# Cross attention of a perceiver block: weighted values of two batches in one TensorE block, and an order of instructions that counts changes of tiling

## The chip, the cores and the metric

The kernel runs on one core of one Trainium2 chip. Its time is the device time of one execution in microseconds (us). Before the change it is 3078.98 us, the median of three runs (3071.81, 3078.98 and 3079.72 us). The engines are called as in the profile: PE is TensorE (PEld its weight loads), ACT is ScalarE, DVE is VectorE, POOL is GpSimd, SP is SyncE, whose queue issues most DMAs.

## The reference, cut to what matters

Six layers run one after the other on `x` (64 batches of 64 rows, 256 wide). The change touches the first one alone, a cross attention from the 64 rows of a batch to the 256 rows of its context, with 16 heads of 16:

```
def _L0_xattn_ref(query, keys, values, mask, Wq, bq, Wk, bk, Wv, bv, Wo, bo):
    q = (query @ Wq.T + bq)   # 64 batches x 64 rows, 16 heads of 16
    k = (keys @ Wk.T + bk)    # 64 batches x 256 rows
    v = (values @ Wv.T + bv)
    energy = einsum('bhqd,bhkd->bhqk', q, k)
    energy = where(mask == 0, -1e20, energy)
    attention = softmax(energy / 4, axis=-1)
    out = einsum('bhqk,bhkd->bhqd', attention, v)
    return out @ Wo.T + bo
x = x + _L0_xattn_ref(layernorm(x), ctx, ctx, mask, ...)
```

The five layers after it (a second attention, a cell of six small attentions, a third attention, a recurrence, a feed-forward layer) are computed in stages 2 to 4, whose code is the same in both kernels.

## The kernel before, in words

**Stages and planner.** The kernel has four stages, and stage 1 is the cross attention. Each stage is written as Python generators ("threads"), and a small planner, `Sched`, decides at build time in which order their steps are issued. A thread yields a request: an engine with a duration in ns (`PE(n, cols)`, `ACT(n)`, `DVE(n)`, `POOL(n)`, `Q(kb)` for a DMA), a buffer of a pool, or an event. The planner keeps a model time for each engine. In `run` it takes, among the requests that can start, the one with the earliest model start; ties go to the lower `prio`. A later one with a better `prio` goes first if that `prio` is better by more than `margin` and it could start within `ahead` (a tenth in stage 1) of the first one's duration. The order that results is fixed: on the chip each engine runs its list in that order, and semaphores make it wait where data or a buffer is not there.

**Tilings.** The matmuls of stage 1 come in three tilings of the array: `PE` is the whole array (projections, transposes), `PR` uses four row groups of 32 (scores: heads' products with 32 contraction rows), `PC` four column groups of 32 (weighted values). `switch` (line 63) gives what the planner charges for a change of tiling: `s.change`, 0 in stage 1 before the change. In `run`, `aware` adds that charge to a candidate's start `t` before it is compared, and `stick` is added to the sorting key `d` for those candidates that would change the tiling:

```
t = max(t, self.eng[self.OF[o[0]]]) + self.aware * self.switch(o[0])
d = t + self.stick * (self.switch(o[0]) > 0)
cand.append(((d, th.prio, d + o[1]), th, o, t))
```

**A unit.** Stage 1 runs over 32 units of two batches. `unit(u)` (prio 10u + 1) loads the context rows, transposes them (line 385), makes keys and values (`values`, lines 344 to 346 by way of `mm3`), and `keep` stores the transposed context for a later stage. `qgroup` makes the queries of two units. `attend(u)` (prio 10u + 2) spawns `batch(u, 0)` and `batch(u, 1)`, then transposes the result (line 790), divides by the softmax sums (796, 797), transposes again (801), and multiplies by the output weights (`mm3`).

**A batch.** `batch` makes the scores twice. First scores: four mask matmuls (line 712) and eight score matmuls (715), then the row maximum on DVE (719). The maximum is negated and split (723, 724), transposed (727) and copied (730). Second scores, now with keys along the partitions: four matmuls that add the negated maximum (736), sixteen of scores (741), then two exponentials on ACT (753) into `pT`. Then it waits for the unit's values and multiplies: 32 matmuls (line 765) of 128 x 32 weights with 64 columns into the first 256 columns of a PSUM buffer of the pool `b1`, and one copy of 128x256 to the half of `o` that belongs to this batch (769, on ACT or DVE, whichever the planner finds free first). An fp32 matmul shows as two instructions in the trace, so these 32 show as 64.

**Buffers.** The scores have one PSUM buffer (`scp`, four of the eight banks): a scores block can begin only when the maximum or the two exponentials of the block before have read it. `b1` has the four other banks. `pT` has three buffers. Work for stage 2 (`prepare2`, prio 100, context projections) is planned among the units from about the tenth on; it changes the tiling too, as half of its matmuls have 64 contraction rows, but the planner counts them as `PE`.

Of the kernel before, what the change touches and what calls it, by code (L numbers as in the profile page):

```python
# [186 lines left out]
def PE(n, cols=512):  # L187
    return "PE", n * PE_NS.get(cols, max(108.7, cols / 2.4))
# [6 lines left out]
def ACT(n, ap=0):  # L195

    return "ACT", 0.833 * n + 55 + 93 * ap


def DVE(n, ap=0):  # L200
    return "DVE", 1.042 * n + 66 + 61 * ap
# [6 lines left out]
def POOL(n):  # L208
    return "POOL", 2.9 * n + 30


def Q(kb=64, wait=True):

    return "Q", 640.0, kb * 2.84, wait
# [82 lines left out]
def f(ap):  # L297
    return ap.bitcast(F32)
# [41 lines left out]
def mm3(k, out, lhs, rhs, start=True, stop=True):  # L340

    n = len(lhs)
    for i, ((ah, al), (bh, bl)) in enumerate(zip(lhs, rhs)):
        k.nc.tensor.matmul(out, ah, bh, start=start and i == 0, stop=False)  # L344
        k.nc.tensor.matmul(out, ah, bl, start=False, stop=False)  # L345
        k.nc.tensor.matmul(out, al, bh, start=False, stop=stop and i == n - 1)  # L346
# [134 lines left out]
def stage1(k, x_in, x_out, ctx, ctxT, mask, wq, bq, wk, bk, wv, bv, wo, bo, beside, nu=32):  # L481
# [1 line left out]


    nc, tc, s = k.nc, k.tc, k.s
    s.ahead, s.margin = 0.1, 4
    es = ExitStack()
    with es:
        pool = lambda name, bufs, **kw: es.enter_context(tc.tile_pool(name=name, bufs=bufs, **kw))
# [4 lines left out]
        b1 = Buf(k, es, "b1", P1["b1"], [128, 512], F32, PSUM)  # L494
        def weight(tp, n, w):
            W[n] = yield from load_wT(k, wp, tp, b1, "w" + n, w, 256, 256)
            s.set(wev[n])
# [94 lines left out]
        ptp = Buf(k, es, "pT", P1["pT"], [128, 2, 4, 2, 128])  # L592
# [11 lines left out]
        def either(n, ap, act, dve):  # L604
            if (yield [ACT(n, ap), DVE(n, ap)]) == "ACT":
                act()
            else:
                dve()
# [94 lines left out]
        rows = [slice(32 * i, 32 * i + 32) for i in range(4)]  # L703
        two = [slice(32 * i, 32 * i + 2) for i in range(4)]

        def batch(u, b, o):
            g, gb = u // 2, 2 * (u % 2) + b
            q_, k_ = qm[g], kc[u]

            sc = yield from scp.on(("PR", 1350))  # L710
            for i in range(4):
                nc.tensor.matmul(sc[:, i], ones[two[i]], mr[g][two[i], gb].unsqueeze(1).to_broadcast([2, 2, 256]), start=True, stop=False)
            for m in range(2):
                for i in range(4):
                    nc.tensor.matmul(sc[:, i, 256 * m:256 * m + 256], q_[rows[i], m, gb].rearrange("p q s -> p (q s)"),  # L715
                                     k_[rows[i], m, 256 * b:256 * b + 256], start=False, stop=m == 1)
            mx = sp.tile([128, 2, 4], F32, name="mx")
            yield DVE(2048)
            nc.vector.tensor_reduce(mx, sc.rearrange("p i (m s) -> p m i s", m=2), AX.X, ALU.max)  # L719
            scp.rel()  # L720
            nx = yield from nxr.get()
            yield "DVE", 200
            nc.vector.tensor_scalar(nx[:, :, :, 0], mx, -1.0, None, ALU.mult)
            nc.vector.scalar_tensor_tensor(nx[:, :, :, 1], mx, -1.0, f(nx[:, :, :, 0]), ALU.mult, ALU.subtract)
            ps = yield from b1.on(PE(2, 128))
            for m in range(2):
                nc.tensor.transpose(ps[:, 128 * m:128 * m + 128], f(nx[:, m].rearrange("p i r -> p (i r)")), k.ident)
            nr = yield from nrp.get()
            pv, nv = ps[:, 0:256], nr.rearrange("p m s -> p (m s)")
            yield from either(256, 0, lambda: nc.scalar.copy(nv, pv), lambda: nc.vector.tensor_copy(nv, pv))  # L730
            b1.rel()
            nxr.rel(k, nx)

            sc = yield from scp.on(("PR", 1350))
            for i in range(4):
                nc.tensor.matmul(sc[:, i], ones[two[i]], nr[two[i]].unsqueeze(1).to_broadcast([2, 2, 2, 128]), start=True, stop=False)
            for c in range(2):
                for m in range(2):
                    for i in range(4):
                        x0 = 256 * c + 128 * m  # L740
                        nc.tensor.matmul(sc[:, i, x0:x0 + 128], k_[rows[i], m, 256 * b + 128 * c:256 * b + 128 * c + 128],  # L741
                                         q_[rows[i], m, gb].rearrange("p q s -> p (q s)"), start=False, stop=c == 1 and m == 1)
            nrp.rel()
            if b == 1:
                kcp.rel()
            qleft[g] -= 1
            if qleft[g] == 0:
                qmp.rel()
                mrp.rel()
            pT = yield from ptp.get()  # L750
            for c in range(2):
                yield ACT(1024, 1)
                nc.scalar.activation(pT[:, c].rearrange("p i m s -> p i (m s)"), sc[:, :, 256 * c:256 * c + 256], AF.Exp,  # L753
                                     bias=W["mc"][:, c, 2 * u + b:2 * u + b + 1], scale=0.25)
            scp.rel()
            yield vready[u]
            v = vv[u]

            av = (yield from b1.on(("PC", 1300)))[:, 0:256].rearrange("p (a s) -> p a s", a=4)
            for a in range(4):  # L760
                for c in range(2):
                    for j in range(4):
                        h = 4 * a + j
                        x0 = 64 * (h % 2)
                        nc.tensor.matmul(av[rows[j], a], v[:, 2 * b + c, h], pT[:, c, h // 2 % 4, h // 8, x0:x0 + 64],
                                         start=c == 0, stop=c == 1, tile_position=(0, 32 * j))
            ptp.rel()
            ov = o[:, :, b]
            yield from either(256, 0, lambda: nc.scalar.copy(ov, av), lambda: nc.vector.tensor_copy(ov, av))
            b1.rel()  # L770

        def attend(u):
            yield qready[u // 2]
            yield kready[u]
            yield mready[u // 2]
            xo = yield from xop.get()
            yield Q(128, False)
            k.dma(xo, x_in[u * 128:(u + 1) * 128])
            yield wev["o"]
            yield POOL(256)  # L780
            nc.gpsimd.tensor_tensor(xo, xo, W["br"], ALU.add)
            o = yield from otp.get()
            ths = [s.spawn(batch(u, b, o), prio=s.curprio() + 0.1 * b) for b in range(2)]
            for t in ths:
                yield t
            vvr.rel(k, vv[u])

            ps = yield from b1.on(PE(4, 128))
            for a in range(4):
                nc.tensor.transpose(ps[:, 128 * a:128 * a + 128], o[:, a].rearrange("p b s -> p (b s)"), k.ident)  # L790
            otp.rel()
            pv = ps.rearrange("p (h d) -> p h d", d=32)
            r = sp.tile([128, 16], F32, name="r")
            on = yield from op.get()
            yield "DVE", 480
            nc.vector.reciprocal(r, pv[:, :, 16])
            nc.vector.tensor_tensor(on, pv[:, :, 0:16], r.unsqueeze(2).to_broadcast([128, 16, 16]), ALU.mult)
            b1.rel()
            ps = yield from b1.on(PE(2, 128))
            for c in range(2):  # L800
                nc.tensor.transpose(ps[:, 128 * c:128 * c + 128], on[:, 8 * c:8 * c + 8].rearrange("p h d -> p (h d)"), k.ident)
            op.rel()
            ohl = yield from ohp.get()
            oh, ol = ohl[:, 0], ohl[:, 1]
            yield from split_ps(k, oh, ol, ps[:, 0:256].rearrange("p (c s) -> p c s", c=2), 256)
            b1.rel()
            wh, wl = W["o"]
            ps = yield from b1.on(PE(6, 256))
            mm3(k, ps[:, 0:256], [(oh[:, c], ol[:, c]) for c in range(2)], [(wh[:, c], wl[:, c]) for c in range(2)])
            ohp.rel()  # L810
            yield DVE(256)
            nc.vector.tensor_tensor(xo, ps[:, 0:256], xo, ALU.add)
            b1.rel()
            yield Q(128)
            k.dma(x_out[u * 128:(u + 1) * 128], xo)
            xop.rel()
            s.set(k.done1[u])

        def main():
# [6 lines left out]
            for t in ths:  # L826
# [6 lines left out]
        ths = [s.spawn(g, prio=p) for g, p in ((weight(tp, "k", wk), -1), (heads(tp), 0), (weight(tp, "v", wv), 1.2),  # L833
                                               (masks(tp), 1.4), (output(tp), 2.5))]
# [1491 lines left out]
```

## Time and profile before

| | us |
|---|---|
| median of three timed runs | 3078.98 |
| profiled execution, time of the run | 3068.5 |
| its span, first to last instruction | 3066.6 |
| stage 1, from the start to the last output matmul at about 668.7 | 668.7 |
| first scores block starts | 36.7 |
| last scores block starts | 659.1 |
| PE busy, share of the span | 2825.0 (92%) |

Besides the page, the profile answers with groups of instructions by line in a window, busy time in stretches, waits (who waited for whom), and a timeline of instructions in order of time. A matmul's duration is its time through the array, so the time that it costs is read from the distance of two starts and not from its duration. In the timeline consecutive matmuls of one line are merged into one row, and a row's second column runs to the end of the last of them. The granted TensorE clock was 1.00 from 64.2 to 671.8 us.

### The profile page before, as it was taken

The numbers are of one execution on the slowest core, as the hardware profiler recorded it, in microseconds if no ns is written. First come the engines' busy times: TensorE is split into PE (matmuls) and PEld (weight loads), VectorE is DVE, ScalarE is ACT, GpSimd is POOL, SyncE is SP. The second block draws the span as 40 slices with busy tenths as digits, with TensorE's granted clock in tenths as the row PEclk, the third lists the DMA queues.
The fourth block names the chain that finished last, engine by engine and source line by source line (L and its number), as shares of the span: only waits on it lengthen the run. The fifth ranks groups of instructions, "written<-read, shape, count | busy, mean of one in ns | idle before, by whom it ended". The sixth has DMA issues, their size and how long they took to land. (4 is left out here: it accounts for less than half of the span.)

```text
span 3066.6 us, 85592 instructions
## 1 busy us (share of the span) xinstructions
PE 2825.0 (92%) x36849; PEld 2283.0 (74%) x36849; DVE 2278.8 (74%) x3430; ACT 1854.2 (60%) x2849; POOL 1032.0 (34%) x1512
## 2 busy tenths in 40 slices
PE   8999999979999999999998998998889899778888
PEld 7877787856666667666667888988888899556767
DVE  6766665558898888987885787888888778776664
ACT  5554455547776776876774565666556566445553
POOL 3110121124554544544451125234523522441220
PEclk9999999999999999999999999999999999889999
DMA  4433452239998999989995456556555656652220
GB/s 149 126 109 100 131 175 71 72 88 222 179 189 187 203 200 191 203 180 175 172 192 126 114 124 148 138 138 160 148 113 134 144 119 164 165 202 83 76 76 22
DMA packets 916987, 437.66 MB, mean 143 GB/s; under 512 B 774264, under 2 KB 884464, under 8 KB 916352
## 3 DMA queue, kind: packets, MB, share of 16 engines
q1 hardware_dynamic: 916608, 432.18, 60.0%
q8 instruction: 290, 4.75, 0.6%
q14 instruction: 89, 0.73, 0.1%
HBM read 183.30 MB, written 64.23 MB: 81 GB/s over the span
## 5 line engine op out<-in xcount | busy, mean ns | idle before, releaser
L1122 ACT ACTIVATE e<-sc,mx,cst 128x1024 f32<-128x1024 f32 x256 | 306.7, 1199 | 118.5 <-POOL mx L1118 116.6
L1624 POOL TENSOR_TENSOR e<-e,sm 128x1024 f32<-128x1024 f32 x96 | 187.7, 1956 | 500.8 <-DVE sm L1622 347.2
L1131 DVE SCALAR_TENSOR_TENSOR p<-e,rs,p 128x1024 f16<-128x1024 f32 x256 | 326.7, 1288 | 38.9 <-ACT p L1129 37.9
L1116 DVE TENSOR_REDUCE mx<-sc 128x1 f32<-128x1024 f32 x256 | 309.2, 1218 | 55.5 <-PE sc L346 54.6
L1129 ACT ACTIVATE p<-e,rs 128x1024 f16<-128x1024 f32 x256 | 289.2, 1145 | 63.7 <-POOL rs L1126 55.1
L1118 POOL TENSOR_SCALAR mx<-mx,cst 128x1 f32<-128x1 f32 x256 | 179.1, 700 | 260.7 <-DVE mx L1116 257.6
L1180 PE MATMUL av<-pT,vv 128*128 128x256 f16 x1536 | 184.8, 278 | 21.3 <-DMA pT<-p 21.1
L1180 PEld LDWEIGHTS <-vv 128*128 128x128 f16 x1536 | 151.2, 100 | 56.3 <-DMA pT<-p 12.5
L719 DVE TENSOR_REDUCE mx<-sc 128x8 f32<-128x2048 f32 x64 | 146.4, 2288 | 62.2 <-PE sc L715 62.0
L1180 PE MATMUL av<-pT,f 128*128 128x256 f16 x1536 | 181.8, 274 | 10.0 <-DMA pT<-p 8.9
L1180 PEld LDWEIGHTS <-f 128*128 128x128 f16 x1536 | 150.1, 98 | 37.4 <-DMA pT<-p 10.3
L753 ACT ACTIVATE pT<-sc,mcol 128x1024 f32<-128x1024 f32 x128 | 139.0, 1115 | 62.8 <-PE sc L741 62.8
L670 POOL TENSOR_TENSOR cT<-chl 128x1024 f32<-128x1024 f32 x32 | 76.4, 2388 | 256.5 <-issue 174.2
L1126 POOL TENSOR_TENSOR rs<-rs,mone 128x1 f32<-128x1 f32 x256 | 154.1, 602 | 21.3
L364 POOL TENSOR_SCALAR ln_rs<-ln_mv 128x1 f32<-128x1 f32 (+2 forms) x136 | 39.2, 288 | 333.9 <-DVE ln_mv L362 310.3
L1125 POOL TENSOR_SCALAR rs<-rs 128x1 f32<-128x1 f32 x256 | 77.4, 302 | 188.7 <-ACT e L1122 177.9
L460 DVE COPY pT<-pX 128x1024 uint16<-128x1024 uint16 x110 | 119.2, 1098 | 22.6 <-DMA pX<-p 22.2
L458 ACT COPY pT<-pX 128x1024 uint16<-128x1024 uint16 x82 | 111.7, 1362 | 37.9 <-DMA pX<-p 37.2
L1618 ACT ACTIVATE e<-e 128x1024 f32<-128x1024 f32 x96 | 101.5, 1058 | 48.8 <-DVE e L1615 48.3
L1621 DVE TENSOR_REDUCE sm<-e 128x16 f32<-128x1024 f32 x96 | 116.5, 1214 | 19.3 <-ACT e L1618 18.8
L1648 PE MATMUL sc<-pT,vn 64*32 64x64 f32 x6144 | 83.6, 227 | 46.2 <-ACT pT L458 12.0
L1612 DVE TENSOR_REDUCE mx<-sc 128x16 f32<-128x1024 f32 x96 | 115.8, 1206 | 13.7 <-PE sc L1606 5.8
(580 smaller groups left out, 9552.9 us busy)
## 6 DMA issues: line engine op xcount, KB each, us to landing
cn<-in_ctx SPq DMA_DIRECT2D x64, 512.0 KB
f<-wdr SPq DMA_DIRECT2D x60, 512.0 KB
wt<-wdr SPq DMA_DIRECT2D x60, 512.0 KB
ctxT<-cT SPq DMA_DIRECT2D x32, 512.0 KB
cT<-ctxT SPq DMA_DIRECT2D x32, 512.0 KB
wdr<-xh SPq DMA_DIRECT2D x30, 512.0 KB
x<-xo SPq DMA_DIRECT2D x64, 128.0 KB
nate<-in_L_ffn_We SPq DMA_DIRECT2D x18, 256.0 KB
```

Source lines behind the costliest of these rows:

```text
L460: k.nc.vector.tensor_copy(out, in_)
L719: nc.vector.tensor_reduce(mx, sc.rearrange("p i (m s) -> p m i s", m=2), AX.X, ALU.max)
L753: nc.scalar.activation(pT[:, c].rearrange("p i m s -> p i (m s)"), sc[:, :, 256 * c:256 * c + 256], AF.Exp, bias=W["mc"][:, c, 2 * u + b:2 ...
L1116: nc.vector.tensor_reduce(mx, sc, AX.X, ALU.max, negate=True)
L1118: nc.gpsimd.tensor_scalar(mx, mx, esc, None, ALU.mult)
L1122: nc.scalar.activation(e, sc, AF.Exp, bias=mx, scale=esc, accum_out=rs)
L1126: nc.gpsimd.tensor_tensor(rs, rs, mone, ALU.pow)
L1129: nc.scalar.activation(p[:, 0], e, AF.Copy, scale=rs)
L1131: nc.vector.scalar_tensor_tensor(p[:, 1], e, rs, p[:, 0], ALU.mult, ALU.subtract)
L1180: nc.tensor.matmul(out, vv[h][:, c, b], pT[:, a, c], start=n == 0, stop=n == 23)
L1621: nc.vector.tensor_reduce(sm, e, AX.X, ALU.add)
L1624: nc.gpsimd.tensor_tensor(e, e, sm.unsqueeze(3).to_broadcast([128, 4, 4, 64]), ALU.mult)
```

## The change

`batch` ends after the exponentials and leaves its `pT` in a dictionary. A new thread step, `weighted`, runs in `attend` when both batches are done: it waits for the unit's values, takes one `b1` buffer, does the 32 matmuls of batch 0 and then the 32 of batch 1 into all 512 columns of it, and copies 128x512 in one instruction. The planner is told 2300 ns for it where it was told 1300 ns for each batch. The number and shapes of the matmuls are the same.

The first line of the stage gives the planner new settings: `margin` 0 for 4, and a charge of 150 ns for a change of tiling, which is part of a candidate's start (`aware`), with `stick` -150. The durations told for scores (1350) stay.

```
-    s.ahead, s.margin = 0.1, 4
+    s.ahead, s.margin, s.aware, s.change, s.stick = 0.1, 0, True, 150, -150
...
-        def batch(u, b, o):
+        def batch(u, b, pts):
...
             scp.rel()
+            pts[b] = pT
+
+        def weighted(u, pts, o):
+
             yield vready[u]
             v = vv[u]
-            av = (yield from b1.on(("PC", 1300)))[:, 0:256].rearrange("p (a s) -> p a s", a=4)
-            for a in range(4):
...
-            ptp.rel()
-            ov = o[:, :, b]
-            yield from either(256, 0, lambda: nc.scalar.copy(ov, av), lambda: nc.vector.tensor_copy(ov, av))
+            ps = yield from b1.on(("PC", 2300))
+            av = ps.rearrange("p (a b s) -> p a b s", a=4, b=2)
+            for b in range(2):
+                for a in range(4):
+                    for c in range(2):
+                        for j in range(4):
+                            h = 4 * a + j
+                            x0 = 64 * (h % 2)
+                            nc.tensor.matmul(av[rows[j], a, b], v[:, 2 * b + c, h], pts[b][:, c, h // 2 % 4, h // 8, x0:x0 + 64],
+                                             start=c == 0, stop=c == 1, tile_position=(0, 32 * j))
+                ptp.rel()
+            ov = o.rearrange("p a b s -> p (a b s)")
+            yield from either(512, 0, lambda: nc.scalar.copy(ov, ps), lambda: nc.vector.tensor_copy(ov, ps))
             b1.rel()
...
-            ths = [s.spawn(batch(u, b, o), prio=s.curprio() + 0.1 * b) for b in range(2)]
+            pts = {}
+            ths = [s.spawn(batch(u, b, pts), prio=s.curprio() + 0.1 * b) for b in range(2)]
             for t in ths:
                 yield t
+            yield from weighted(u, pts, o)
```

## The prediction

> **What bounds it now.** I read the page first, for the slices, then the busy time in stretches of stage 1, then the waits and timeline there. Stage 1 ends near 668.7 us of a span of 3066.6; in the page's slices that is about the first nine digits.
>
> ```profile
> span 3066.6 us, 85592 instructions
> ...
> PE   8999999979999999999998998998889899778888
> ...
> DVE  6766665558898888987885787888888778776664
> ACT  5554455547776776876774565666556566445553
> ```
>
> In the next answer the columns are the stretch, its length, and the busy time of PE, PEld, DVE, ACT and POOL.
>
> ```profile
> 60.00:561.60 501.60, 490.92 (x7864) 394.20 (x7862) 314.66 (x542) 266.73 (x423) 87.51 (x75) 1.00 0.37 117
> 561.60:596.70 35.10, 34.19 (x619) 28.82 (x612) 18.61 (x27) 19.55 (x31) 6.21 (x4) 1.00 0.23 78
> 640.00:668.60 28.60, 19.17 (x475) 15.46 (x468) 8.96 (x17) 11.01 (x15) 0.10 (x1) 0.92 0.04 12
> ```
>
> PE is busy 98% of the time from 60 to 561.6, ACT 53% and DVE 63%. So PE's list bounds the stage, and what counts is PE's own work plus its few waits. 561.6 to 596.7 is two units without work of stage 2: 17.55 us a unit. The last 28.6 us are a tail in which nothing is left to fill PE.
>
> The waits from 60 to 668 have these two as the longest (total us, times, longest); together with the same two on DVE's maximum (3.7 and 2.3) they are 16.2 us.
>
> ```profile
> PE sc L736 <- ACT pT L753: 7.1, 9, 1.5
> ...
> PE sc L712 <- ACT pT L753: 3.1, 4, 1.3
> ```
>
> PE waits for the one scores buffer. The durations that hold it, from the groups by line:
>
> ```profile
> L719 DVE TENSOR_REDUCE mx<-sc 128x8 f32<-128x2048 f32 x62 | 141.8, 2288 | 62.1 <-PE sc L715 62.0
> L753 ACT ACTIVATE pT<-sc,mcol 128x1024 f32<-128x1024 f32 x124 | 134.7, 1115 | 60.8 <-PE sc L741 60.8
> ```
>
> Either 2.29 us, or twice 1.115 us, lies between two scores blocks, and PE needs other work meanwhile. The timeline shows both sides (start, duration to the last end, idle before):
>
> ```profile
> 607.14 1.04 PE L385 MATMUL b<-ident,cn 128*128 128x128 f32 x8
> 608.83 0.50 PE L736 MATMUL sc<-nr,ones 2*128 2x512 f32 x4 [0.66 <-ACT pT L753]
> 609.17 1.06 PE L741 MATMUL sc<-qm,kc 32*128 32x128 f32 x32
> 610.16 1.10 PE L765 MATMUL b<-pT,vv 128*32 128x64 f32 x64
> 611.19 1.09 PE L385 MATMUL b<-ident,cn 128*128 128x128 f32 x8
> 612.54 0.51 PE L712 MATMUL sc<-mr,ones 2*128 2x512 f32 x4 [0.25 <-ACT pT L753]
> ```
>
> Two second-scores blocks follow each other at 4.06 us, then a first-scores block at 3.71. The weighted values of batch 0 (L765) are fill here, and even with them PE ran dry.
>
> **Merging the weighted values.** A block of 64 instructions costs 1.03 us (610.16 to 611.19). By the single starts in the trace, groups of four start 0.056 us apart, so 16 groups are 0.90 us and 0.135 us is the price of the block: 0.04 at its beginning and 0.09 behind its last group.
>
> ```profile
> 630.28 0.40 PE L345 MATMUL b<-chl,wkh 128*128 128x512 f32 x1
> 630.51 0.40 PE L346 MATMUL b<-chl,wkl 128*128 128x512 f32 x1
> 630.84 1.10 PE L765 MATMUL b<-pT,vv 128*32 128x64 f32 x64
> 631.87 0.51 PE L712 MATMUL sc<-mr,ones 2*128 2x512 f32 x4
> ```
>
> The 0.09 is the change of tiling: siblings start 0.23 apart (630.28, 630.51), the first one of the other tiling 0.33 later. The same 0.09 stands behind scores blocks (0.200 to the next block, where groups are 0.112 apart). From 60 to 668 us I count 61 blocks of weighted values. 55 of their 122 sides touch a scores block; there the array would have changed anyway. So they add 122 - 55 = 67 changes. Afterwards there are 32 blocks with 64 sides. If all stand alone they add 64 changes (3 fewer, 0.3 us), if each touches one scores block 32 (35 fewer, 3.2 us); at today's share of 45% they add 35 (32 fewer, 2.9 us). The 0.04 goes 32 times: 1.3 us. **PE's own work falls by 1.6 to 4.5 us; I take 4.2.** The scores blocks number 128 as before.
>
> **One eviction.** Today 46 copies on ACT at 0.372 us and 18 on DVE at 0.424: 24.7 us. Copies of 128x512 in the same stage (values, line 661) take 0.586 on ACT and 0.689 on DVE; 23 and 9 of them are 19.7. Both engines save 5.0 us together, beside PE's list: nothing on the path. It comes 0.21 to 0.27 us later for the transposes behind it, which wait for it 1.0 us in all today; in the tail there is no cover, so 0.2 us once.
>
> The Trainium skill, "TensorEngine Tiling (Array Packing)", Performance Considerations, PSUM Bottleneck, speaks against this edit: it wants both ScalarE and VectorE to empty PSUM, and one wide copy lets only one do so. The row bears on it with 0.372 against 0.586; if the transposes stood on the path, the rule would make it 32 x 0.21 = 7 us lost, and by the waits it is nothing.
>
> **The added wait.** Batch 0's weighted values used to be issued while batch 1's exponentials ran, and were fill (610.16 above). Now they come behind batch 1's exponentials. Behind them on PE is whatever the planner put there, above all the next unit's first scores. No DMA and no other queue is touched; SP and POOL get nothing new. Two `pT` stay held for some 4 us longer, and the third is free for the next unit's batch 0, so no new wait there.
>
> What it costs depends on who goes first when the exponentials end. Three distances of a unit's four are 3.80, 4.0 and 4.05 at their shortest, and the fourth is 3.71 if the next scores go first. Then the chain through the scores buffer is 15.6 us a unit, below PE's work (17.55 less the 0.45 of waits, 1.8 us in four units, less 0.13: 16.97), and the waits vanish: 0.58 a unit gained here. Over the stage that is at most the 8.8 us that PE waits at lines 712 and 736 from 60 to 630 us. If the merged block goes first, the chain is 15.6 + 1.93 = 17.5, above PE's work: 0.05 gained. In the trace the weighted values precede the next first scores in 25 units of 32 and follow them in 7. The code says why: the scores' start has no latency on the buffer's release, the weighted values' has 250 ns, but a PE that is still filling makes them equal, and then the lower prio, the older unit's, wins. Some 23 units lie outside the work of stage 2, nine inside, where PE has fill and gains its 0.13. **All first: 23 x 0.05 + 9 x 0.13 = 2.3 us gained; all behind: 8.8 + 4.2 = 13.0; weighed 25 to 7: 4.6, so 5.**
>
> **The settings.** They add and remove no instruction. `stick` of -150 takes the 150 out of the key again, so the order is not pulled towards fewer changes; only the planner's clock runs slower. `margin` 0 lets values of a unit precede its own scores within a tenth of a block. Scores cost 1.30 to 1.33 us plus 0.09, 1.42; they were charged 1.35 and are now charged up to 1.65. The merged block costs 2.0 and is charged up to 2.6. Against that, a projection of 512 columns is charged 0.213 and takes 0.23. Over a unit today's plan is 16.65 us against 17.55 real; the new one adds 4 x 0.30 = 1.2, 17.85 against some 17. Errors in both directions of like size: I take 0, with rival 2 below as one end and the 8.8 us of waits, all gone, as the other.
>
> **Sum.** 5 us off: 3068.5 - 5 = 3063.5 for the profiled execution (span 3066.6 and 1.9 around it). The three timed runs have their median 10.5 above it, so 3079.0 - 5 = 3074.0. About 0.3% (9.2 us) is what a measurement of this kernel can tell from no change.
>
> **Rivals.** (1) *Next scores go first.* The chain drops out and 13 us are gained, 3066. For it: the 250 ns, and seven units today. Against it: a full PE hides the 250 ns. (2) *The plan believes in a slower PE than the chip has.* Then the planned fill between two scores blocks is too short and PE waits at lines 712 and 736. Surplus in the fill per unit: 4 x 0.12 (two changes at 150 for 90) + 0.5 (merged block) = 1.0; projections charged too low give back 8% of some 8.6 us fill, 0.7. It decides from the point where the planned fill is down to the wait itself, as at 607.14. 0.3 x 32 = 10 us, 3089; without the giving back 32 us. (3) *The change doesn't do what it says:* the order is as before, apart from the merging, and only the 1.6 to 4.5 us come; that lies in the forecast. Stages 2 to 4 inherit other model times at stage 1's end, so their order can shift a little; I allow 5 us to either side.
>
> **Chances.** Forecast with (3), within 0.3%: 0.46. Rival 1, faster: 0.34. Rival 2, slower: 0.20. The range: down to rival 1 with 5 us of later stages and 5 of scatter between runs, 3056; up to rival 2 with 2 more, 3091. The forecast's own range is 3067 to 3081.
>
> **What would show it.** L765 in 32 blocks of 128, each about 1.93 us to the next start; copies at line 769's successor 0.59 or 0.69; 128 scores blocks; some 30 fewer changes of tiling. Units without stage 2's work at 17.4 to 17.5 us (rival 1: 17.0; rival 2: 17.8 and more, with waits of PE at 712 and 736 well over 16 us). It would be wrong if stage 1 shrank and a later stage grew, or if the tail of 28.6 us changed by more than 1 us.

## The result, and the profile after

| | before | after |
|---|---|---|
| median of 20 timed runs each, us | 3078.6 (3070.8 to 3085.2) | 3083.1 (3078.3 to 3096.9) |
| profiled execution: time, span, us | 3068.5, 3066.6 | 3082.8, 3081.0 |
| last output matmul of stage 1, us | 669.1 | 671.3 |
| mean granted clock | 0.980 | 0.975 |

The ratio is 1.0019, with a 95% interval of 1.0010 to 1.0028: 0.2% slower, within the 0.3% that one measurement can tell from no change, but with 20 runs on each side clearly not the 5 us faster that were forecast. The two profiled executions lie 14 us apart; before's lies 10 us under its median. Two executions of kernels that end behind stage 1 (2039.6 us of after, 2037.8 us of merging alone) took three times as long as the others of the same kernel and are left out of the medians below.

The page of the changed kernel first (slices of 77.0 us; stage 1 is the first nine). PE's first nine digits are those of before, so the answer must be in shorter stretches.

```profile
span 3081.0 us, 85536 instructions
...
PE   8999999979999999999988999999999899778888
```

The stretches that answer to those of before (length; busy time of PE, PEld, DVE, ACT, POOL; granted clock, DMA share, GB/s). The last is a stretch of the same 28.6 us at the stage's end, moved with it.

```profile
60.00:561.60 501.60, 489.70 (x7751) 395.83 (x7749) 302.14 (x534) 264.61 (x409) 92.16 (x76) 1.00 0.38 118
561.60:596.90 35.30, 34.35 (x614) 28.91 (x614) 19.05 (x31) 17.72 (x27) 6.61 (x5) 1.00 0.18 63
642.60:671.20 28.60, 20.12 (x446) 16.05 (x443) 9.43 (x17) 10.93 (x14) 0.10 (x1) 0.88 0.04 12
```

PE is busy 97.6% of the time from 60 to 561.6, nearly as before (97.9%), two units without work of stage 2 take 35.3 us where they took 35.1, and the clock of the last 28.6 us is 0.88 where it was 0.92. The waits of PE from 60 to 668 us (total us, times, longest):

```profile
PE sc L712 <- ACT pT L753: 6.5, 5, 2.3
PE sc L736 <- DVE mx L719: 4.9, 6, 1.7
PE sc L712 <- DVE mx L719: 3.4, 8, 0.5
PE sc L736 <- ACT pT L753: 3.2, 5, 1.3
PE b L770 <- ACT pT L753: 2.2, 3, 1.2
PE b L770 <- issue: 1.6, 2, 1.4
```

The four scores rows add up to 18.0 us, against 16.2 before, and two rows are new, of the merged block (line 770; the lines behind the change are shifted by up to 7): 2.2 us for exponentials, and 1.6 in the middle of two blocks that the profile puts down to nothing ("issue"). The wait for the scores buffer has not gone. What moved is its place. The single copy of 128x512 is there as well, always on ACT:

```profile
L774 ACT COPY ot<-b x32: 585/585/588, 55.3 to 667.1; 128x512 f32<-128x512 f32 x32
```

**How stage 1 divides.** The next table is worked out from the traces, and most of what follows rests on it. "Start" is the first scores block; the body runs from there to the first scores of the 61st batch, the tail from there to the stage's last output matmul. "Idle" is time with no matmul in PE. "Half clock" is time with a granted clock of 0.5 (half of it is taken as lost). "Own work" is the body less its idle time less half of its half-clock time. Each row is a mean over the profiles of all runs with that stage 1, whole or cut off behind it.

| stage 1 (profiles) | start | body | own work | idle | half clock | tail | tail's half clock | end |
|---|---|---|---|---|---|---|---|---|
| before (5) | 37.2 | 595.3 | 578.6 | 15.4 | 2.7 | 38.0 | 8.7 | 670.6 |
| after (4) | 35.5 | 596.4 | 576.6 | 17.8 | 3.9 | 39.7 | 12.3 | 671.5 |
| merging alone (2) | 38.1 | 596.8 | 574.6 | 19.7 | 5.1 | 39.5 | 10.8 | 674.3 |
| settings alone (4) | 35.6 | 592.9 | 579.7 | 12.0 | 2.6 | 37.0 | 4.1 | 665.4 |
| late, not merged (1) | 38.5 | 594.3 | 580.1 | 12.5 | 3.4 | 38.1 | 3.4 | 670.8 |
| behind (1) | 34.9 | 612.0 | 572.5 | 29.2 | 20.5 | 41.5 | 14.9 | 688.4 |
| charge alone (1) | 36.7 | 612.5 | 582.4 | 25.0 | 10.2 | 41.6 | 20.5 | 690.7 |
| margin alone (1) | 35.3 | 607.1 | 578.1 | 22.2 | 13.7 | 41.0 | 18.4 | 683.4 |

Own work and idle time repeat within 1 to 2 us from profile to profile of one kernel; the half-clock time does not (before's tail has 4.8 to 11.8 us). Of the kernels that end behind stage 1, the profiled execution of after, of merging alone and of settings alone was the longest of those timed, so the ends of these three rows lie rather late.

### The profile page after: what moved, and what is told of

It is laid out like the page before. It is cut to its first block, busy times and chain, and to the rows that moved or that the text cites. A ratio compares the mean times of both kernels' runs of the same rounds, so it can differ in the third digit from the quotient of the medians.

```text
span 3081.0 us, 85536 instructions
## 1 busy us (share of the span) xinstructions
PE 2831.8 (92%) x36849; PEld 2292.2 (74%) x36849; DVE 2267.3 (74%) x3428; ACT 1846.5 (60%) x2819; POOL 1037.2 (34%) x1512
## 5 line engine op out<-in xcount | busy, mean ns | idle before, releaser
L1136 ACT ACTIVATE p<-e,rs 128x1024 f16<-128x1024 f32 x256 | 289.2, 1145 | 67.1 <-POOL rs L1133 56.7
L1187 PE MATMUL av<-pT,f 128*128 128x256 f16 x1536 | 184.4, 276 | 12.5 <-DMA pT<-p 11.9
L1187 PEld LDWEIGHTS <-vv 128*128 128x128 f16 x1536 | 151.0, 100 | 57.8 <-DMA pT<-p 13.7
L458 ACT COPY pT<-pX 128x1024 uint16<-128x1024 uint16 x82 | 111.7, 1362 | 35.9 <-DMA pX<-p 35.5
L460 DVE COPY pT<-pX 128x1024 uint16<-128x1024 uint16 x110 | 117.8, 1085 | 20.3 <-DMA pX<-p 19.7
L1619 DVE TENSOR_REDUCE mx<-sc 128x16 f32<-128x1024 f32 x96 | 115.7, 1206 | 13.8 <-PE sc L1613 5.9
```

The source lines that it names most:

```text
L460: k.nc.vector.tensor_copy(out, in_)
L1136: nc.scalar.activation(p[:, 0], e, AF.Copy, scale=rs)
L1187: nc.tensor.matmul(out, vv[h][:, c, b], pT[:, a, c], start=n == 0, stop=n == 23)
L1619: nc.vector.tensor_reduce(mx, sv, AX.X, ALU.max)
```

## The experiments

**Each half alone.** The merged block with the old settings, the new settings with weighted values batch by batch, and the kernel before once more as a control, all beside the kernel before (29 runs, median 3079.3).

```
-    s.ahead, s.margin, s.aware, s.change, s.stick = 0.1, 0, True, 150, -150
+    s.ahead, s.margin = 0.1, 4
```

> The merged block alone, with the planner's settings of before (margin 4, no charge for a change of tiling). Theory A (the merged block is the loss: the fill of batch 0's weighted values is gone and 1.93 us stand ahead of the next scores, so the chain through the scores buffer is as long as PE's work, and in the tail PE idles and its clock falls): stage 1 ends 1 to 3 us later than before (669.1), some 671; time +0 to +0.2%. Theory B (the settings are the loss, the merging gains what was worked out): stage 1 ends 4 to 5 us earlier, 664 to 665, time -0.15%. Theory C (stage 1 is equal, the difference is scatter of the later stages): stage 1 within 1 us of 669.

Measured: 3084.8 us (12 runs, 3080.2 to 3091.9), ratio 1.0016 [1.0007, 1.0024]. Merging alone makes the kernel slower, though PE's own work in stage 1 falls by 4.0 us (578.6 to 574.6). Stage 1 ended at 674.4 us in its profile, later than any of the three theories had it; theory A has the direction.

> The settings alone (margin 0, charge 150 in the start, stick -150), weighted values batch by batch as before. Theory A: stage 1 within 1 us of 669. Theory B: 6 us later or more, some 675, with more waits of PE at lines 712 and 736 than the 16 us of before; time +0.2% or more. Theory C: within 1 us of 669.

Measured: 3081.2 us (12 runs, 3071.9 to 3086.1), ratio 1.0003 [0.9992, 1.0014]: no difference in full time, though stage 1 ends some 5 us earlier (664.0 in its profile). None of the three theories expected that.

> The kernel before, once more, as a measure of scatter: ratio 1.000 within 0.1%. Stage 1 ends at 669.1 within 1 us in every theory; the rest of the span (2397.5 in the first profile, 2409.7 in the changed kernel's) shows how far stages 2 to 4 scatter when nothing is changed. Theory C expects a spread of 5 us and more there.

Measured: 3079.7 us (12 runs), ratio 1.0001 [0.9992, 1.0010]. Its profile has the same order as the one shown and yet a span of 3072.7 against 3066.6. Two profiles of one kernel can lie 6 us apart, so single spans decide nothing here.

**Rival 1 forced: next scores first.** The merged block becomes a thread of its own with a prio behind the next unit's scores.

```
-            yield from weighted(u, pts, o)
+            yield s.spawn(weighted(u, pts, o), prio=s.curprio() + 10.5)
```

> The changed kernel with the merged block in a thread of its own whose prio is worse than that of both batches' scores of the next unit (10.5 more), so that it is fill between scores blocks instead of standing ahead of them. Theory A: units without stage 2's work fall from 17.6 to about 17.0 us, waits at 712 and 736 before 630 us fall from 9.9 to under 5, stage 1 ends 6 to 10 us earlier than the changed kernel's 671.3, at 661 to 665. Theory B (too slow a clock in the plan): the waits stay, stage 1 within 2 us of 671.

Measured: 3093.4 us (6 runs, 3084.8 to 3102.2), ratio 1.0044 [1.0028, 1.0061]. In its order the merged block stands behind the next unit's first scores in 23 units and ahead in 8, of the 31 that have a next unit, where after has 11 and 20. The waits did not vanish: idle time of the body is 29.2 us, the highest of all, and stage 1 ends at 688.4 us, far behind what either theory expected.

**Stage 1 by itself.** The kernel ends behind stage 1, whose result is written out; stages 2 to 4 are left out. The work for stage 2 that is planned among the units stays.

```
-        ps[2] = prepare2(k, x1, *g("L0_attn_", "context Wq Wk Wv Wout bout"))
+        ps[2] = prepare2(k, xo, *g("L0_attn_", "context Wq Wk Wv Wout bout"))
...
-    stage1(k, x0, x1, a["ctx_1024"], ctxT, a["mask_BxS2_ik0"], *g("L0_xattn_", "Wq bq Wk bk Wv bv Wo bo"), before2)
-    stage2(k, x1, x2, ps[2], before3)
-    stage3(k, x2, x3, ps[3], before4, last3)
-    stage4(k, x3, xo, a["ctx_1024"], ctxT, ps[4])
+    stage1(k, x0, xo, a["ctx_1024"], ctxT, a["mask_BxS2_ik0"], *g("L0_xattn_", "Wq bq Wk bk Wv bv Wo bo"), before2)
+    k.e2.close()
```

> The kernel before, cut off after stage 1 (stages 2 to 4 are left out, stage 1 writes to the output). This and the next three time stage 1 alone, without the scatter of the 2400 us behind it. In the two full profiles stage 1 ended at 669.1 and 671.9; I expect a time of 671 to 675 with a spread of about 2 us. Both theories use it as the base.

> The changed kernel, cut off after stage 1 in the same way. Theory D (stage 1 itself is longer, and that is the whole of the +4.5 us): 4 to 5 us over the cut kernel before. Theory E (stage 1 is nearly equal, as the profiles have it, and most of the loss comes behind it although the instructions there are the same): 0 to 2 us over it.

> The new settings alone, weighted values batch by batch, cut off after stage 1. Theory D: equal to the cut kernel before within 2 us, as the full times were. Theory E: 5 to 7 us under it, as the profile of the full kernel has it, so that the gain is lost behind stage 1.

> The merged block alone with the old settings, cut off after stage 1. Theory D: 5 to 6 us over the cut kernel before, as the full times were; theory E: 3 to 5 us over it, as the profile has it.

Measured (medians of four or five): before 675.5 (674.8 to 676.0), after 673.9 (673.0 to 676.1), settings alone 671.7 (670.3 to 675.1), merging alone 678.6 (677.4 to 679.5). (The expectations further down were written with 674.5 and 678.8, medians that counted the two long executions, and so with 2.8 for the cost of merging.) So in stage 1 the settings gain 3.8 us with the old block (675.5 to 671.7) and 4.7 with the merged one (678.6 to 673.9); the merging costs 3.1 with the old settings and 2.2 with the new ones. After is 1.6 us ahead of before here, so the 4.5 us of full time are not lost in stage 1: theory D has fallen, and theory E is the nearer one.

**Up to the end of stage 2.** As before, with stage 2 kept and stages 3 and 4 left out.

```
+    stage1(k, x0, x1, a["ctx_1024"], ctxT, a["mask_BxS2_ik0"], *g("L0_xattn_", "Wq bq Wk bk Wv bv Wo bo"), before2)
+    stage2(k, x1, xo, ps[2], before3)
```

> The kernel before, cut off after stage 2 (stages 3 and 4 are left out, stage 2 writes to the output). With the full times (before 3079.3, after 3083.1, settings alone 3081.2) and the cuts after stage 1 (675.5, 674.5, 671.7), 5 us of the change's loss lie behind stage 1. Base of the next two; I expect 1650 to 1670.

> The changed kernel, cut off after stage 2. Theory E1 (the loss behind stage 1 lies at the start of stage 2, where SyncE's queue and the transfers of pT have a pace of their own and the profiles show 3.6 us lost up to 120 us into the stage): 3 us and more over the cut kernel before. Theory E2 (it lies in stage 3): 1 us under it to 1 us over it, as after stage 1.

> The settings alone, cut off after stage 2. Theory E1: the 3.8 us gained in stage 1 are gone, within 1 us of the cut kernel before. Theory E2: they are still there, 3 to 4 us under it.

Measured: 1643.7 (1637.5 to 1645.0), 1645.3 (1641.1 to 1647.2), 1629.9 (1629.5 to 1631.7). After is 1.6 us behind, with ranges that overlap, so E1 and E2 are not told apart; the settings alone are 13.8 us ahead here, which neither expected, and yet 2 behind at the end of the kernel. Of the 12.3 us between the two profiled spans 8.5 stood at the end of stage 1 already (672.3 and 663.8); where the rest was gained was not traced.

**Up to the end of stage 3.** Stage 4 alone is left out.

```
-    stage3(k, x2, x3, ps[3], before4, last3)
-    stage4(k, x3, xo, a["ctx_1024"], ctxT, ps[4])
+    stage3(k, x2, xo, ps[3], before4, last3)
```

> The kernel before without stage 4 (the recurrence's output is written out instead). It gives the base for the two others of this call: full time 3079 less stage 4's 361 us and the end's, some 2712 to 2722.

> The changed kernel without stage 4. Theory S (the loss of some 5 us behind stage 1 arises in stage 3, with the same instructions, from TensorE's granted clock, which falls at different moments): 4 us above the kernel before cut in the same way, since it stood 1.6 above at the end of stage 2. Rival L (it arises behind stage 3): within 2 us of it.

> The kernel with the new settings and weighted values batch by batch, without stage 4. At the end of stage 2 it stood 13.8 us below before, in full time 1.9 above. Theory S: the 14 to 16 us are lost again in stage 3, so it lies within 3 us of the kernel before cut in the same way, in all of its timed runs. Rival L: some 13 us below.

Measured: 2723.7 (2723.3 to 2727.6), 2729.7 (2726.9 to 2731.1), 2726.0 (2715.1 to 2735.7). Rival L has fallen: after has lost 6.1 us by the end of stage 3 against 1.6 at the end of stage 2, and the settings alone have given all of their 13.8 back by the median. By these medians both go in stage 3. Theory S asked that all runs of the settings alone lie within 3 us of before; they lie from 8.6 below to 12.0 above it.

**The tail.** The last two units with weighted values batch by batch, the others merged; cut off behind stage 1.

```
+            if u < nu - 2:
+                return
+            yield vready[u]
...
-            yield from weighted(u, pts, o)
+            if u < nu - 2:
+                yield from weighted(u, pts, o)
```

> The changed kernel cut off after stage 1, with the weighted values of the last two units batch by batch as before. Theory F (half of the 2.8 us that merging costs under the new settings comes from the tail, where PE idles 2.3 us before two scores blocks and its clock is halved for 6.8 us): 671.5 to 673.5 against 674.5, the tail behind the 60th batch's first scores 37 to 38 us against 39.5. Against it (the tail is bound by the scores buffer alone): 674 to 675.

Measured: 676.5 us (673.0 to 679.0) against 673.9: no gain. The trace says why this run can't decide: both gaps of 2.31 us ahead of the next first scores are still there (632.66 and 650.12). The first needs the block of the third unit from the end, which is still merged in this run. Into the second the planner did not put batch 0's block; it stands ahead of the second scores at 646.41 and delays them.

**The wait without the merging.** Weighted values wait for both batches, but stay two blocks with two copies; old settings; cut off behind stage 1.

```
+            for b in range(2):
+                av = (yield from b1.on(("PC", 1300)))[:, 0:256].rearrange("p (a s) -> p a s", a=4)
...
-            ps = yield from b1.on(("PC", 2300))
```

> The kernel is cut off behind stage 1, with the old settings; the weighted values wait for both batches as after the change, but stay two blocks of 64 with two copies of 128x256. Theory W (the wait costs, the merging saves as forecast): the kernel lacks the some 4 us of PE's work that one block per unit saves, and has the late batch 0, so it lies some 7 us above before's 675.5, at 681 to 684, and some 4 above the merged one's 678.8. Rival E (the wide block is the trouble: 1.93 us that fit badly between two scores blocks, and a copy of 0.59 us): about before's 675.5, within 1.5. Rival N (the late batch 0 costs 3 and the merging saves nothing that reaches the end): within 1 of 678.8.

Measured: 675.5 us (674.2 to 676.1), the same as before. Theory W has fallen, and so has rival N: the wait of batch 0 costs nothing on balance, and what costs is the wide block (with its one copy, and with 2300 ns told for it in place of twice 1300, which this run does not separate from it). The waits of PE in the body, from 36 to 631 us, first of the merged kernel, then of the one with two late blocks:

```profile
PE sc L712 <- ACT pT L753: 6.3, 9, 1.9
PE b L770 <- issue: 3.3, 2, 2.6
```

```profile
PE sc L736 <- DVE mx L719: 3.6, 7, 1.0
PE sc L712 <- ACT pT L753: 3.4, 7, 1.3
```

With two blocks PE has no wait at the weighted values, and the next first scores wait half as long for the exponentials. Own work is 580.1 against 574.6 (the merging saves 5.5 here), idle time 12.5 against 19.7.

The idle time of the body can be sorted by what PE has between two scores blocks (us, in brackets the number of such stretches; one profile each, the first three of kernels that end behind stage 1):

| between two scores blocks | before | two late blocks | merging alone | settings alone | after | behind |
|---|---|---|---|---|---|---|
| weighted values between two first-scores blocks | 0.0 (5) | 0.2 (27) | 4.7 (15) | 0.0 (3) | 4.2 (9) | 13.0 (22) |
| second scores, then first scores, no weighted values between | 1.3 (2) | 5.1 (16) | 7.8 (16) | 2.0 (4) | 4.8 (10) | 6.7 (22) |
| all other stretches | 14.2 | 7.2 | 6.9 | 9.7 | 8.4 | 9.5 |

Lateness has its price in the second row, where the weighted values are missing, and two narrow late blocks make it good elsewhere. What the merged block adds is above all the first row. Not all of that is lack of fill: 2.6 us of the 4.7 and 1.4 of the 4.2 are a single stop inside a merged block that the profile puts down to nothing.

**The settings one by one.** Weighted values as before the change, cut off behind stage 1.

```
-    s.ahead, s.margin = 0.1, 4
+    s.ahead, s.margin, s.aware, s.change, s.stick = 0.1, 4, True, 150, -150
```

> Cut off behind stage 1; weighted values as before the change; of the settings the charge of 150 with its -150 in the key alone, margin 4 as before. If the slower clock of the planner is what gains (it plans less fill between two scores blocks than PE has room for, so the scores come earlier): 671.7 within 1, as with both settings. If it is the margin: 675.5 within 1.

```
-    s.ahead, s.margin = 0.1, 4
+    s.ahead, s.margin = 0.1, 0
```

> Cut off behind stage 1; weighted values as before the change; margin 0 alone, no charge. If the charge is what gains: 675.5 within 1. If the margin is what gains: 671.7 within 1. If each gives a part, the two parts of this run and the one with the charge alone add up to 3.8.

Measured: 695.0 us (693.4 to 696.4) and 690.1 us (688.6 to 691.7), against 675.5 with neither and 671.7 with both. None of the three expectations holds: alone they cost 19.5 and 14.6, together they gain 3.8. With the charge alone the body has 9.6 us more idle time than before's, 3.8 more own work, 3.8 more lost to half clock, and the tail is 3.6 longer. The idle time isn't spread evenly (start, duration, idle before):

```profile
362.16 0.41 PE L801 MATMUL b<-ident,o 128*128 128x128 f32 x2 [1.82 <-DVE o L797]
364.26 0.80 PE L712 MATMUL sc<-mr,ones 2*128 2x512 f32 x4 [1.70 <-DVE mx L719]
364.86 1.91 PE L715 MATMUL sc<-kc,qm 32*128 32x256 f32 x16
```

Two gaps in a row with only two transposes between them, and then the clock is halved: the block at line 715 shows 1.91 us where it shows 1.03 at full clock. With the margin alone the body's longest gap is 5.8 us, the weighted values waiting for a DVE that is busy elsewhere, and again half clock behind it:

```profile
PE b L765 <- DVE xo L812: 5.8, 1, 5.8
```

With 6.8 and 10.2 us of half clock behind them, these places alone cost some 7 and 11 us. Why the two settings are harmless together was not traced further.

## Why the prediction was wrong, point by point

**What bounds the stage: right.** PE is busy 97.6% of the time from 60 to 561.6, and the table divides every kernel above into PE's own work, its idle time and its half clock.

**Merging the weighted values, 4.2 us less work: right in size, by the old settings.** The merged block takes 1.925 us to the next start (median of the undisturbed ones) where two took 2 x 1.03; the forecast had 1.93. Changes of tiling from 60 to 668 us fell from 377 to 327, 50 fewer where some 30 were forecast (the forecast's count set the 61 narrow blocks of that stretch, of 64, against all 32 merged ones). Own work fell by 4.0 us with the old settings and by 3.1 with the new ones (579.7 to 576.6). The new settings themselves add 1.1, which the forecast had at nothing, so that 2.0 of the 4.2 are left between before and after. More changes went than forecast and less time, so 0.09 us for each is not a price that can be multiplied through the stage.

**One eviction, nothing on the path: right.** 32 copies at 0.585 us, and the transposes waited for them once, 0.7 us, where before they waited twice, 1.0 us in all. The doubled length of one engine's copy, against which a rule was weighed, cost nothing measurable.

**"The added wait ... 2.3 us gained ... 13.0 ... weighed 25 to 7: 4.6, so 5": the step that failed.** By the table the body's idle time rose by 4.3 us with the old settings (15.4 to 19.7) and by 5.8 with the new ones (12.0 to 17.8). The forecast had 4.6 gained, 4.2 of it work, so an idle time that falls by 0.4, and rises by 1.9 in its worst case of all blocks ahead. In the timed kernels that end behind stage 1 the merging, with its work and its wait, cost 3.1 and 2.2 us where 5 were to be gained. Lateness in itself costs nothing on balance (12.5 idle with two late blocks, less than before). Of the 31 merged blocks that have a next unit 20 stand ahead of its first scores and 11 behind them. The forecast's way of counting makes that 21 to 11, for which its own weighing gives 6.0 gained, so the order that came is not what it missed. What it left out is that a block of 1.93 us is one piece: by the traces it is either in the way of the next scores or missing as fill, and it can't stand half in one gap and half in the next. In a unit of the second kind (the profile after; start, duration):

```profile
598.19 1.99 PE L770 MATMUL b<-pT,vv 128*32 128x64 f32 x128
600.68 0.50 PE L712 MATMUL sc<-mr,ones 2*128 2x512 f32 x4 [0.49 <-DVE mx L719]
```

The block is the only fill for the maximum's 2.29 us, and PE is dry for 0.49. That comes five times in the body of after and fourteen times in that of rival 1's run, where the forecast had the waits vanish. In the units of the first kind the block comes on top of a full stretch, and the scores distance there is 6.26 us where 4.0 is the need. Two units then take 35.2 to 35.3, as before. At the end of the body the lack is larger, since there are no projections left to fill:

```profile
627.52 0.51 PE L736 MATMUL sc<-nr,ones 2*128 2x512 f32 x4 [0.77 <-ACT pT L753]
631.23 0.80 PE L712 MATMUL sc<-mr,ones 2*128 2x512 f32 x4 [2.31 <-ACT pT L753]
633.67 3.64 PE L770 MATMUL b<-pT,vv 128*32 128x64 f32 x128
```

At this place before had batch 0's weighted values (630.84 in the forecast's rows) and no gap. The last eight scores blocks ahead of the tail hold 4.1 us of idle time after the change and 0.9 before, which is more than the whole rise between the two kernels (2.4). That the wide block, and not the wait, is what costs is shown by the run with two late blocks for the old settings; for the new settings it was not run. How much of it is the one piece, and how much the stops inside merged blocks (3.3 us in the run with the old settings, 1.6 after the change), stays open.

**The tail would change by less than 1 us: wrong, 1.7.** (The forecast's tail begins at 640, the table's at the 61st batch, some 8 us earlier.) Its idle time is the same (10.2, before 9.2 to 10.4). Its half-clock time is longer by 3.6 us, which is worth 1.8: the gap above is followed by half clock from 630.8 to 637.6, and the merged block takes 3.64 us in it. Busy time and clock there:

```profile
630.80:637.60 6.80, 6.37 (x152) 5.28 (x156) 2.64 (x3) 0.60 (x2) 0.14 (x1) 0.50 0.02 5
```

Before had half clock in its tail too: the section on time and profile before has 1.00 from 64.2 to 671.8 us, but counted from the span's start, as all other times here, full clock runs from 53.3 to 660.9, and half clock follows to 664.3 and again from 667.7.

**"The settings ... Errors in both directions of like size: I take 0": wrong by 4 to 5 us, in the kernel's favour, and wrong in kind.** They gain 3.8 us in the timed kernels that end behind stage 1 (4.7 with the merged block) and 5.2 in the profiles, 3.4 of it idle time and 1.6 at the start. But the sum of believed prices that the step made says nothing about this: each of the two settings alone moves the same stage by 15 to 20 us the other way. A sum of over- and undercharged prices is no model of what an order does.

**The rivals.** Rival 1 (next scores first, 13 us gained) was forced and lost 14 us. Own work fell to 572.5, but idle time and half clock rose by more, for want of further fill beside the merged block (13.0 us in the sorted table's first row). Rival 2 (the plan believes in a slower PE, 10 lost) isn't what happened: the full settings make the stage shorter; and where the charge alone loses, PE waits at lines 712 and 736 for 11.5 us from 36 to 631, before 10.4, so it isn't the thin loss in each unit that was priced. Rival 3 (only the merging comes, some 4 gained) is refuted by the merging alone, 1.0016 [1.0007, 1.0024].

**Later stages, "5 us to either side", at nothing in the sum: 6.1 us, for another reason, and they decide the sign.** After is 1.6 us ahead at the end of stage 1 and 4.5 behind at the end of the kernel; the forecast had named "if stage 1 shrank and a later stage grew" as a sign of being wrong. They "inherit other model times", the forecast said, "so their order can shift a little". The order didn't shift: from stage 2 on each engine has the same instructions in the same order in before, after, and the two halves alone. Still after is 4.5 us further behind at the end of stage 3 than at the end of stage 2 (6.1 less 1.6). Stage 3's own stretch, from the last weighted values of stage 2 to its last node, in the profiles of before, after and the settings alone (length; PE's busy time and number of matmuls; granted clock in the column before the last two):

```profile
1620.60:2701.10 1080.50, 971.63 (x18509) 900.35 (x18507) 864.33 (x1326) 622.30 (x1005) 369.16 (x392) 0.98 0.57 136
```

```profile
1627.60:2715.20 1087.60, 978.10 (x18509) 906.60 (x18507) 864.45 (x1326) 621.67 (x1005) 368.87 (x393) 0.97 0.57 135
```

```profile
1616.50:2712.70 1096.20, 984.67 (x18509) 913.47 (x18508) 866.06 (x1328) 623.05 (x1005) 370.48 (x395) 0.96 0.57 134
```

The same 18509 matmuls take 6.5 and 13.0 us longer while DVE and ACT take the same time within 2 us, and the clock column goes with it: half clock for 50.3, 67.1 and 84.1 us. Over the nine profiles that have a stage 3 its length goes with its half-clock time (correlation 0.88, 0.35 us of length for 1 us of half clock): before 1080.5 to 1083.6, after 1087.6 and 1088.2, settings alone 1091.2 and 1096.2. That the time is lost there is shown by the timed kernels, and that half clock goes with it by the profiles. Whether a kernel has its own amount of half clock in stage 3, or nine profiles fell that way by chance, stays open: the order is the same, and the runs of the settings alone up to stage 3 scatter over 20 us.

**Sum.** From the start of the kernel to the end of stage 1, after against before by the table: start -1.7, own work -2.0, idle +2.4, half clock in the body +0.6, tail +1.7, together +1.0; by the timed kernels it is -1.6. Stage 2 makes it +1.6 (a step within the scatter of those runs), stage 3 +6.1, the full kernel +4.5. From the forecast's -5 to +4.5 are 9.5 us: 7.2 for the merging and its wait, which cost 2.2 with the new settings instead of gaining 5, less 3.8 for the settings, and 6.1 for the later stages, both at nothing in the sum. How far the later stages' part comes from the change at all stays open. No version run here beats the kernel before in full time; late blocks with the new settings, or a merged block that is split where it is the only fill, were not tried.

## What to carry to other kernels

Work that is saved on the bounding engine is gained only where the time it leaves is filled again: before merging two blocks of fill into one, look for the places where such a block is the only fill (behind a first-scores block, or at the end of the stage, where other work has run out), and count both the gap and the clock behind it. A planner's settings can't be forecast by adding up its pricing errors; two that lose 15 to 20 us each gained 4 together, so build each and compare the orders. And where stages with the same instructions vary by more than the change, cut the kernel off behind the stage that changed.

## What the runs showed of the hardware

**In these runs TensorE's clock follows how busy each window of 3.41 us was.** In the traces the granted clock changes only on a grid of 3.413 us, which is fixed within a run and lies differently in each. I took each grid window's share of matmul time (ends of matmuls are modelled in the trace, so the shares are too), from the first scores block to the end of stage 1 in all 20 profiles and in stage 3 of nine. Of the windows at full clock with PE busy for less than 0.45, 83 of 83 were followed by a window at half clock; with over 0.65, none of 5913; between them it goes over gradually (49 of 60 at 0.45 to 0.50, 28 of 63 at 0.50 to 0.55, 22 of 182 from there to 0.65). Back to full clock it goes behind a window that was at least some 0.9 busy (144 of 147), in some cases from 0.8 to 0.9 (17 of 31), and below that in 2 of 88. In the profile after, the gap of 2.31 us from 628.9 lies mostly in one window, with 1.40 of 3.41 us busy:

```profile
627.41:630.82 3.41, 1.40 (x36) 1.17 (x36) 0.07 (x1) 1.82 (x3) 0.60 (x1) 1.00 0.18 57
644.47:647.89 3.42, 2.25 (x42) 1.72 (x41) 0.54 (x2) 1.71 (x3) 0.00 (x0) 1.00 0.11 38
647.89:651.30 3.41, 2.27 (x88) 1.86 (x92) 0.82 (x1) 1.09 (x2) 0.00 (x0) 1.00 0.02 5
```

Half clock follows for two windows. An equal gap of 2.31 us from 646.7 is split between the two other windows, 0.66 busy each, and nothing happens. So a gap's price depends on where the grid falls, and the grid lies differently in each run: laying it differently over the same stage 3 of before leaves between 10 and 17 windows less than 0.48 busy. The Trainium skill, "TensorE: Matmul & The Clock Gate", Part 1, has the free-running window of 3413 ns and the two clocks, and the runs agree (3.413 us, 1.0 and 0.5). Its rule that the clock falls after an idle window, or a gap of more than some 3.4 us, differs from these runs, where a window 41% busy was enough; here the measurement decides.

**Identical instructions, 16 us apart.** Stage 3 took from 1080.5 to 1096.2 us with the same order on each engine, as told above. A change of a few us in an early stage can't be read from single spans of such a kernel.
